# A graph step and a mixture of experts in one kernel: ScalarE's follow-up steps up to a slot later, x loads three slots sooner

## The chip, the cores and the metric

The kernel runs on one core of one Trainium2 chip. The metric is device time in microseconds (us) of one execution. TensorE (PE) multiplies matrices, with the weight loads shown as PEld; VectorE (DVE) does elementwise work, reductions and scans; ScalarE (ACT) does activations and copies; GpSimd (POOL) issues the indirect transfers; SyncE (SP) issues most of the plain ones. Each engine executes its own list of instructions strictly in the order in which the program emitted them, so an instruction that waits holds up everything behind it on that engine.

## The reference, cut to what matters

There are 6250 nodes with 256 features, and 100,000 edges with 96 features, sorted by target node. The first half adds a graph step to x, the second half a mixture of experts with two of sixteen experts per node.

```python
h1 = layernorm(x)
s   = segment_sum(edge, dst); m = segment_max(edge, dst); mean = s / max(count, 1)
h   = concat([h1, s, m, mean, u[0]])
x   = x + h1 + relu(h @ W1 + b1) @ W2 + b2
t   = layernorm(x)
val, idx = top_k(t @ gate_w + gate_b, 2);  w = softmax(val)
moe = sum_k w[k] * (relu(t @ w1[idx[k]] + b1[idx[k]]) @ w2[idx[k]] + b2[idx[k]])
out = x + layernorm(t + moe) * gamma + beta
```

With two choices the softmax needs one exponential of the difference of the two best logits (`dv`).

## The kernel before, in words

**Groups and slots.** The nodes are cut into 13 groups of four tiles of 125 nodes (the first group has two). One group's life is spread over slots; group g's multi-layer perceptron starts at slot B = 12 g. A list of tasks `(slot, function)` is sorted once, and that order is the order of emission for all engines. A slot is a place in this list, with a planned length of 4.6 us; it is no time on the chip.

**The edge stream.** Sums and maxima over the edges are no tasks but a generator (`steps`, `edge_stream`) that is drawn from between slots while the planned time allows (`credit`). It cuts the edges into seven regions and those into chunks. For each chunk SP loads edges (`raw`, three buffers, L176), VectorE forms running sums and maxima into `rw` (four operations of 125x768 per step, L316 to L320), and SP stores them to DRAM (`rows_d`, L329). After a region its last rows must be chained: `chain_runs` has three parts. `over_runs` (L385 to L396) chains the eight runs in a partition into the tile `ct`, of which there is one buffer; ScalarE copies the last run into it (L392). `to_features` transposes on TensorE (L404, L406), `over_partitions` scans on VectorE (L415 to L421), `to_partitions` transposes back (L430), `to_runs` adds the carry (L436, L438), and POOL stores `ct` as `carry_d` (L440). Functions given to `for_pe` are kept back until the next slot begins.

**One group around the change.** SP loads x (`take_x`, L680) at slot B-17. VectorE takes mean and variance (`stats_x`, L690, L691), ScalarE the root (`root_x`, L696), VectorE its inverse (`scale_x`, L702), ScalarE normalises (`norm_x`, L710). POOL gathers edge rows (`take_edges`, L730) and carries (`take_carry`, L737) for four tiles, VectorE joins them (`join_edges`, L743, L745), ScalarE scales them (L750, L617, L618), TensorE transposes (`turn`, L763) through a single bank `pT`, and ScalarE copies each out (`inT`, L764). `hidden` (L772, L789) is followed by ScalarE's relu (L794), `output` (L800) by VectorE's `residual` (L805 to L810). Then come the second root (`root_b`, ScalarE, L814), its inverse (`scale_b`, L820), the transposes `turn_b` (L830, copied out by ScalarE as `gT`, L831), `logits` (L838), `choose` on VectorE (L845 to L852) with the exponential on ScalarE at its end (L853), `rank`, `rank_2` (L873, L874), `place` (L882 to L895, which reads the exponential at L891), and `send` (POOL, L899), which scatters the rows to the experts' lists.

**Experts.** After the last group the rows are taken in blocks of 256: up to 14 blocks of one expert first, then 43 others (L1166 and L1190 are the two layers, L1172 and L1170 the relu, L1089 and L1091 the weighting).

**Queues.** SP's queue holds edge loads, stores of rows and x loads in the order of emission. POOL's queue holds the gathers of `blk_i` (L495, which need VectorE's L490 to L492), the sends, the stores of carries and the gathers of rows and carries.

The exponential and the square root belong to different function tables of ScalarE; the program holds a table load (`ACT_TABLE_LOAD`) wherever the table changes, 28 in all.

Of the kernel before, what the change touches and what calls it, by code (L numbers as in the profile page):

```python
# [13 lines left out]
AF = mybir.ActivationFunctionType  # L14
# [7 lines left out]
RR = 8  # L22
# [15 lines left out]
SLOTS = 12  # L38
# [7 lines left out]
def kernel(  # L46
# [18 lines left out]
    nc = tc.nc  # L65
    N, D = x.shape
    E, EF = edge.shape
# [23 lines left out]
    GRP = [(GS * (NG - 1 - g), GS * (NG - 1 - g) + (GS if g else N0)) for g in range(NG)]  # L91
# [126 lines left out]
    early = w1p.tile([P, 2 * WE * EF], F32, name="w1")  # L218
# [117 lines left out]
    def for_pe(fn):  # L336
        deferred.append((clock[0], fn))

    def tell_pe(now=False):

        while deferred and (now or deferred[0][0] < clock[0]):
            deferred.pop(0)[1]()
            told[0] = -1 if now else clock[0]

    def edge_stream():

        parts, of = [], 0

        def next_part():
            for cost in parts.pop(0)():  # L350
                yield cost
            stored[of] = not parts

        def ready():
            return not deferred and (clock[0] < 0 or told[0] < clock[0])

        for cost, whole, end in steps():
            yield cost
            if whole and parts and ready():
                yield from next_part()  # L360
            if end is not None:
                while parts:
                    tell_pe(True)
                    yield from next_part()
                parts, of = chain_runs(end), end
                yield from next_part()
                while parts and end == 0:
                    tell_pe(True)
                    yield from next_part()
        while parts:  # L370
            while not ready():
                yield None
            yield from next_part()
# [4 lines left out]
    def chain_runs(c):  # L378
        prev = prevs.pop(c)
        ct = chp.tile([P, RR, 2 * EF], F32, name="ct")  # L380
        kb, kp, kb2 = (chp.tile([P, RR], F32, name=nm) for nm in ("kbar", "kp", "kbar2"))

        def over_runs():

            nc.vector.tensor_scalar(kb, kall[:, c], 2.0, -1.0, op0=OP.mult, op1=OP.add)  # L385
            nc.vector.tensor_scalar(kb, kb, BIG, None, op0=OP.mult)
            nc.vector.tensor_tensor_scan(kp[:, ::-1], kall[:, c, ::-1], kall[:, c, ::-1], 1.0, op0=OP.mult, op1=OP.min)
            nc.vector.tensor_scalar(kb2, kp, 2.0, -1.0, op0=OP.mult, op1=OP.add)
            nc.vector.tensor_scalar(kb2, kb2, BIG, None, op0=OP.mult)
            run = tuple(a[:, RR - 1, :] for a in prev)  # L390
            for h in range(2):
                nc.scalar.copy(ct[:, RR - 1, h * EF:(h + 1) * EF], run[h])  # L392
            for r in reversed(range(RR - 1)):
                to = ct[:, r, 0:EF], ct[:, r, EF:]
                nc.vector.scalar_tensor_tensor(to[0], run[0], kall[:, c, r:r + 1], prev[0][:, r, :], op0=OP.mult, op1=OP.add)
                nc.vector.scalar_tensor_tensor(to[1], run[1], kb[:, r:r + 1], prev[1][:, r, :], op0=OP.min, op1=OP.max)  # L396
                run = to
                if r % 3 == 0:
                    yield 1.8
            for_pe(to_features)  # L400

        def to_features():
            over_runs.pk = pk = eps.tile([EF, 3, P], F32, name="ps")
            nc.tensor.transpose(pk[:, 0, :], kp[:, 0:1].to_broadcast([P, EF]), ident[:P, :P])  # L404
            for h in range(2):
                nc.tensor.transpose(pk[:, 1 + h, :], ct[:, 0, h * EF:(h + 1) * EF], ident[:P, :P])  # L406

        def over_partitions():
            pk = over_runs.pk
            st = chp.tile([EF, 2, P + 1], F32, name="st", bufs=2)  # L410
            for h in range(2):
                if chain[0] is None:
                    nc.vector.memset(st[:, h, P:], 0.0)
                else:
                    nc.vector.tensor_copy(st[:, h, P:], chain[0][:, h, 0:1])  # L415
            kk = chp.tile([EF, 2, P], F32, name="kk")
            nc.vector.tensor_copy(kk[:, 0, :], pk[:, 0, :])
            nc.vector.tensor_scalar(kk[:, 1, :], kk[:, 0, :], 2.0, -1.0, op0=OP.mult, op1=OP.add)
            nc.vector.tensor_scalar(kk[:, 1, :], kk[:, 1, :], BIG, None, op0=OP.mult)
            for h in range(2):  # L420
                nc.vector.tensor_tensor_scan(st[:, h, P - 1::-1], kk[:, h, ::-1], pk[:, 1 + h, ::-1], st[:, h, P:],  # L421
                                             op0=(OP.mult, OP.min)[h], op1=(OP.add, OP.max)[h])
            chain[0] = st
            yield 2.0
            for_pe(to_partitions)

        def to_partitions():
            over_runs.pc = pc = eps.tile([P, 2 * EF], F32, name="ps")
            for h in range(2):
                nc.tensor.transpose(pc[:, h * EF:(h + 1) * EF], chain[0][:, h, 1:], ident[:EF, :EF])  # L430

        def to_runs():
            tmp = chp.tile([P, RR, EF], F32, name="tmp")
            for h, k, o0, o1 in ((0, kp, OP.mult, OP.add), (1, kb2, OP.min, OP.max)):
                cs = ct[:, :, h * EF:(h + 1) * EF]
                nc.vector.tensor_tensor(tmp, over_runs.pc[:, None, h * EF:(h + 1) * EF].to_broadcast([P, RR, EF]),  # L436
                                        k[:, :, None].to_broadcast([P, RR, EF]), op=o0)
                nc.vector.tensor_tensor(cs, cs, tmp, op=o1)  # L438
                yield 1.9
            nc.gpsimd.dma_start(carry_d[EP * c:EP * (c + 1)].rearrange("(p r) f -> p r f", p=P), ct)  # L440

        return [over_runs, over_partitions, to_runs]


# [230 lines left out]
    G = [{} for _ in GRP]  # L675
# [165 lines left out]
    def choose(g):  # L841
        n = GRP[g][1] - GRP[g][0]
        lg = gtp.tile([P, GS, NE], F32, name="lg")
        G[g]["V8"], G[g]["I8"] = V8, I8 = gtp.tile([P, GS, 8], F32, name="V8"), gtp.tile([P, GS, 8], U32, name="I8")
        nc.vector.tensor_tensor(lg[:, :n], G[g]["pL"][:, :n * NE].rearrange("p (i e) -> p i e", e=NE),  # L845
                                G[g]["xt"][:, :n, D + 5:D + 6].to_broadcast([P, n, NE]), op=OP.mult)
        nc.vector.tensor_tensor(lg[:, :n], lg[:, :n], gbs[:, None, :].to_broadcast([P, n, NE]), op=OP.add)
        for i in range(n):
            nc.vector.max(V8[:, i, :], lg[:, i, :])
            nc.vector.max_index(I8[:, i, :], V8[:, i, :], lg[:, i, :])  # L850
        G[g]["dv"] = dv = gtp.tile([P, GS], F32, name="dv")
        nc.vector.tensor_sub(dv[:, :n], V8[:, :n, 1], V8[:, :n, 0])  # L852
        nc.scalar.activation(dv[:, :n], dv[:, :n], AF.Exp)  # L853

    def rank(g):
        a, z = GRP[g]
# [356 lines left out]
    def at_slot(T, fn, *a, cost=0.0):  # L1213
        tasks.append((T, len(tasks), fn, a, cost))

    stream = edge_stream()
    cuts = []

# [11 lines left out]
    for g, (a, z) in enumerate(GRP):  # L1230
        B, n = SLOTS * g, z - a
# [4 lines left out]
    for g, (a, z) in enumerate(GRP):  # L1236
        B, n = SLOTS * g, z - a
        if g:
            if g > 1:
                at_slot(max(0, B - 17), take_x, g)  # L1240
                after = 5 if g == GW else 0
                at_slot(B - 14 + after, stats_x, g, 0, cost=1.2)
                at_slot(B - 13 + after, stats_x, g, 1, cost=1.2)
# [4 lines left out]
            for i in range(n):  # L1248
                if g >= GW:
                    late = 3 if g == GW else 0  # L1250
# [19 lines left out]
        for i in range(n):  # L1270
            at_slot(B + HC + 1 + i, residual, g, i, cost=1.1)
        early = GS - n
        at_slot(B + SLOTS + 1 - early, root_b, g)
        at_slot(B + SLOTS + 2 - early, scale_b, g, cost=0.3)
        late = 0 if g >= NG - 2 else 1
        for k in range(DC):
            at_slot(B + SLOTS + 1 + k, turn_b, g, k)
        at_slot(B + SLOTS + 3 + late, logits, g)
        at_slot(B + SLOTS + 4 + late, choose, g, cost=2.4)
        at_slot(B + SLOTS + 5 + late, rank, g, cost=1.3)  # L1280
        at_slot(B + SLOTS + 6 + 2 * late, rank_2, g)
        at_slot(B + SLOTS + 7 + 2 * late, place, g, cost=1.5)
        for i in range(n):
# [20 lines left out]
    for b in range(GW, len(IB)):  # L1304
# [11 lines left out]
        early = 0 if b == GW else 2  # L1316
# [80 lines left out]
    with tc.If(bad_v != 0):  # L1397
# [7 lines left out]
        for lo in range(0, N, NC):  # L1405
# [18 lines left out]
            for n0 in range(0, min(NC, N - lo), P):  # L1424
                n = min(P, NC - n0, N - lo - n0)
# [14 lines left out]
    with tc.manual_schedule():  # L1440
# [56 lines left out]
        for slot, _, fn, args, cost in tasks:  # L1497
            while slot > T:
# [6 lines left out]
                g = min(T // SLOTS, NG - 1)  # L1505
# [61 lines left out]
```

## Time and profile before

| what | value |
|---|---|
| median of three runs | 1291.13 us (1291.03 to 1294.33) |
| the profiled execution, its own time | 1299.43 us |
| its span, first to last instruction | 1297.6 us |
| PE / DVE / ACT / POOL busy over the span | 1113.4 / 963.4 / 612.6 / 558.8 us |
| mean granted clock of TensorE | 0.955 |
| PE and DVE busy from 110 to 728 us, out of 618 | 538.9 and 547.1 us |
| PE and DVE busy from 728 to 806 us, out of 78 | 76.4 and 23.8 us |

The profiled execution took 8.3 us longer than the median of the other three. The span falls into the preparation (to about 110 us), the groups with the edge stream (to about 728 us), the last groups without it (to about 806 us) and the experts. In the tables a line such as `ACT dv L853 <- DVE dv L852: 75.2, 8, 16.2` says that ScalarE sat idle before line 853 until VectorE's line 852 had ended, 75.2 us in total, 8 times, at most 16.2 us. In the timeline, `[4.97 <-DMA ...]` is the idle time before an instruction and what ended it.

### The profile page before, as it was taken

The page shows a single profiled execution, that of the slowest core. Times are in us where ns is not written, and L with a number is a line of the kernel's source. Part 1 is how long each engine was busy: PE and PEld are TensorE (multiplying, and loading weights), DVE is VectorE, ACT ScalarE, POOL GpSimd, SP SyncE. Part 2 cuts the span into 40 slices and gives each one's busy share as a digit, 9 for nine tenths or more (in the row PEclk, how much of TensorE's full clock was granted, in tenths as well). Part 3 has the DMA queues.
Part 4 walks back from the last instruction along what each step waited for, and adds up shares of the span by engine and source line. Part 5 has one row for each costly group of instructions (what it writes and reads, how often), then busy time and mean ns, then how long its engine had stood idle before and what let it go on. Part 6 is the DMA issues. An engine that isn't in the chain of part 4 may idle for free.

```text
span 1297.6 us, 16883 instructions
## 1 busy us (share of the span) xinstructions
PE 1113.4 (86%) x4637; PEld 783.4 (60%) x4637; DVE 963.4 (74%) x2754; ACT 612.6 (47%) x1449; POOL 558.8 (43%) x721
## 2 busy tenths in 40 slices
PE   2484796998789989899989999998999998989992
PEld 1252363655455554646646566886888777778881
DVE  4569787988988979999989422444377777778885
ACT  3484253662437542343424422432466666656662
POOL 4121142663347645375263333030145554545664
PEclk9897898999889998999999999998999999999996
DMA  5948785797779998898997331231677777778972
GB/s 163 209 108 234 206 242 160 204 242 208 216 222 267 252 244 228 235 255 228 274 260 237 90 95 42 66 100 50 195 229 228 231 238 252 254 228 254 280 259 73
DMA packets 179475, 261.25 MB, mean 201 GB/s; under 512 B 35915, under 2 KB 145963, under 8 KB 173729
## 3 DMA queue, kind: packets, MB, share of 16 engines
q1 hardware_dynamic: 140241, 202.23, 54.4%
q0 software_dynamic: 39008, 57.35, 16.1%
q8 instruction: 40, 0.66, 0.2%
q14 instruction: 74, 0.61, 0.2%
q10 hardware_dynamic: 112, 0.41, 0.1%
HBM read 146.70 MB, written 122.01 MB: 207 GB/s over the span
## 4 chain that ended last, share of the span: by engine, by line
PE 35%; DVE 13%; ACT 3%; DMA 3%; issue 3%; POOL 1%; POOLq 0%; SPq 0%; ACTq 0%; DVEq 0%
PE acc L1190 14%; PE acc L1166 11%; PE acc L772 5%; PE acc L800 3%; DVE yb L1089 2%; ACT yb L1091 2%; DVE rw L320 1%; DVE rw L317 1%; DVE rw L319 1%; DVE rw L316 1%; DMA xt<-in_x_dram 1%; ACT hb L1172 1%; DMA cg<-carry_d,next_i 1%; DMA xg_d<-xt,pos_i 1%; POOL xg_d L899 1%
## 5 line engine op out<-in xcount | busy, mean ns | idle before, releaser
L772 PE MATMUL acc<-inT,w1x 128*128 128x500 f32 (+1 forms) x832 | 369.0, 592 | 8.9 <-DVE xt L805 8.9
L772 PEld LDWEIGHTS acc<-inT,w1x 128*128 128x128 f32 x832 | 159.0, 199 | 169.7 <-issue 151.9
L1166 PE MATMUL acc<-xT,wt 128*128 128x256 f32 x912 | 223.2, 388 | 29.3 <-ACT hb L1172 25.7
L899 POOL DMA_INDIRECT xg_d<-xt,pos_i x100 | 134.4, 1344 | 250.2 <-DVE xt L895 119.8
L1190 PE MATMUL acc<-wt,hb 128*128 128x256 f32 x912 | 207.1, 380 | 0.0
L1166 PEld LDWEIGHTS acc<-xT,wt 128*128 128x128 f32 x912 | 169.2, 191 | 62.3 <-ACT hb L1172 38.1
L1190 PEld LDWEIGHTS acc<-wt,hb 128*128 128x128 f32 x912 | 174.1, 191 | 23.9
L800 PE MATMUL acc<-w2s,hT 128*125 128x256 f32 x800 | 186.5, 388 | 0.0
L800 PEld LDWEIGHTS acc<-w2s,hT 128*125 128x125 f32 x800 | 150.5, 193 | 23.7 <-issue 1.9
L1102 POOL DMA_INDIRECT g<-y_d,from_i x86 | 91.8, 1067 | 120.8 <-DMA y_d<-yb 90.5
L1135 POOL DMA_INDIRECT out_dram<-g,to_i x86 | 89.1, 1036 | 102.7 <-ACT hb L1172 86.5
L1091 ACT ACTIVATE yb<-yb,w_b 128x256 f32<-128x256 f32 x114 | 51.7, 501 | 154.0 <-DVE yb L1089 147.8
L495 POOL DMA_INDIRECT gb<-in_dst_dram,blk_i x50 | 74.1, 1483 | 114.2 <-issue 59.4
L1172 ACT ACTIVATE hb<-acc,wt 128x256 f32<-128x256 f32 x200 | 87.7, 464 | 49.5 <-PE acc L1166 41.0
L1089 DVE TENSOR_TENSOR yb<-acc,xe 128x512 f32<-128x512 f32 x57 | 39.4, 691 | 88.3 <-PE acc L1190 57.4
L794 ACT ACTIVATE hT<-acc,c 128x500 f32<-128x500 f32 (+1 forms) x104 | 60.1, 660 | 71.4 <-PE acc L789 71.4
L319 DVE TENSOR_TENSOR rw<-rw,raw 125x768 f32<-125x768 f32 x88 | 83.8, 953 | 0.0
L320 DVE TENSOR_TENSOR rw<-rw,raw 125x768 f32<-125x768 f32 x88 | 83.7, 951 | 0.0
L316 DVE TENSOR_TENSOR rw<-rw,keep 125x768 f32<-125x768 f32 x81 | 76.8, 948 | 5.0 <-DMA rows_d<-rw 4.9
L317 DVE TENSOR_TENSOR rw<-rw,bar 125x768 f32<-125x768 f32 x81 | 77.0, 950 | 0.0
L730 POOL DMA_INDIRECT at<-rows_d,first_i x44 | 61.6, 1399 | 34.2 <-issue 21.5
L737 POOL DMA_INDIRECT cg<-carry_d,next_i x44 | 63.2, 1437 | 25.7 <-issue 11.3
(313 smaller groups left out, 1577.9 us busy)
## 6 DMA issues: line engine op xcount, KB each, us to landing
wt<-in_wpack_dram SPq DMA_DIRECT2D x44, 1026.0 KB
rows_d<-rw SPq DMA_DIRECT2D x46, 960.0 KB
rows_d<-rw SPq DMA_DIRECT2D x46, 540.0 KB
raw<-in_edge_dram SPq DMA_DIRECT2D x46, 480.0 KB
xb<-xg_d SPq DMA_DIRECT2D x57, 263.0 KB
y_d<-yb SPq DMA_DIRECT2D x57, 256.0 KB
raw<-in_edge_dram SPq DMA_DIRECT2D x46, 270.0 KB
xt<-in_x_dram SPq DMA_DIRECT2D x12, 500.0 KB
```

Source lines behind the costliest of these rows:

```text
L316: nc.vector.tensor_tensor(su, prev[0], keep[c][:, :, s + j, None].to_broadcast(bcast), op=OP.mult)
L317: nc.vector.tensor_tensor(mx, prev[1], bar[c][:, :, s + j, None].to_broadcast(bcast), op=OP.min)
L319: nc.vector.tensor_tensor(su, su, x_j, op=OP.add)
L320: nc.vector.tensor_tensor(mx, mx, x_j, op=OP.max)
L772: nc.tensor.matmul(G[g]["pH"][m % 4][:, :n * P], w1x[:, k, m * 128:(m + 1) * 128], inT[:, k, :n * P], start=(k == 0), stop=False)
L800: nc.tensor.matmul(pO, G[g]["hT"][m][:, i * P:(i + 1) * P], w2s[:, m, :], start=(m == 0), stop=(m == HC - 1))
L899: d = nc.gpsimd.indirect_dma_start(out=xg_d[:, :], out_offset=IndirectOffsetOnAxis(ap=G[g]["pos"][:, i, k:k + 1], axis=0), in_=G[g]["xt"][ ...
L1102: d = nc.gpsimd.indirect_dma_start(out=g[:, h, :].bitcast(I32), out_offset=None, in_=y_d[:, :], in_offset=IndirectOffsetOnAxis(ap=BL[b]["f ...
L1135: d = nc.gpsimd.indirect_dma_start(out=out[:, :], out_offset=IndirectOffsetOnAxis(ap=BL[b]["to"][:, h:h + 1], axis=0), in_=g[:, h, :], in_ ...
L1166: nc.tensor.matmul(pB[i][:, half, :], wt[:, k * FF + m * 128:k * FF + (m + 1) * 128], xT[:, k, :], start=(k == 0), stop=(k == DC - 1))
L1172: nc.scalar.activation(hb[:, m, :], pB[i][:, half, :], AF.Relu, bias=bias)
L1190: nc.tensor.matmul(pY[:, h, :], hb[:, m, h * 128:(h + 1) * 128], wt[:, W2O + m * D:W2O + (m + 1) * D], start=(m == order[0]), stop=(m == o ...
```

## The change

Four things move, and nothing is added or taken away on any engine.

- The exponential leaves `choose` and becomes a task of its own, `choose_2`, one slot later in most groups (after `rank`, and half a slot further).
- `root_b` and `scale_b` come one slot later.
- The copies of the last run into `ct` leave `over_runs` and stand at the head of `to_features`, which is emitted when the next slot begins. For the third region (index 2) the first part of the chain is no longer emitted at once, but at the next whole step of the stream.
- `take_x` is listed at slot B-20 instead of B-17.

```diff
                 parts, of = chain_runs(end), end
-                yield from next_part()
+                if end != 2:
+                    yield from next_part()
@@ over_runs
             run = tuple(a[:, RR - 1, :] for a in prev)
-            for h in range(2):
-                nc.scalar.copy(ct[:, RR - 1, h * EF:(h + 1) * EF], run[h])
@@
         def to_features():
+            for h in range(2):
+                nc.scalar.copy(ct[:, RR - 1, h * EF:(h + 1) * EF], prev[h][:, RR - 1, :])
@@ choose
-        nc.scalar.activation(dv[:, :n], dv[:, :n], AF.Exp)
+
+    def choose_2(g):
+        n = GRP[g][1] - GRP[g][0]
+        nc.scalar.activation(G[g]["dv"][:, :n], G[g]["dv"][:, :n], AF.Exp)
@@ the list of tasks
-                at_slot(max(0, B - 17), take_x, g)
+                at_slot(max(0, B - 20), take_x, g)
@@
-        at_slot(B + SLOTS + 1 - early, root_b, g)
-        at_slot(B + SLOTS + 2 - early, scale_b, g, cost=0.3)
+        at_slot(B + SLOTS + 2 - early, root_b, g)
+        at_slot(B + SLOTS + 3 - early, scale_b, g, cost=0.3)
@@
         at_slot(B + SLOTS + 5 + late, rank, g, cost=1.3)
+        at_slot(B + SLOTS + 5 + late + (0.5 if late else 0), choose_2, g)
```

## The prediction

> **What bounds the kernel now.** I read the stages first (busy time by stretch), then who waited for whom in the stretch that the change touches, then the timeline around each wait. The stages, with PE, PEld, DVE, ACT and POOL busy and the instruction counts in brackets:
>
> ```profile
> 110.00:728.00 618.00, 538.89 (x2031) 321.14 (x2030) 547.10 (x1451) 260.49 (x605) 294.47 (x281) 0.94 0.84 229
> 728.00:806.00 78.00, 76.38 (x309) 48.75 (x309) 23.76 (x107) 23.41 (x46) 28.03 (x40) 1.00 0.23 67
> ```
>
> From 728 us TensorE is full and nothing else matters. From 110 to 728 us TensorE and VectorE are both near nine tenths. The waits decide which leads. First VectorE's, then TensorE's and ScalarE's, all from 110 to 728 us:
>
> ```profile
> DVE at L743 <- DMA cg<-carry_d,next_i: 23.6, 14, 5.4
> DVE bsa L690 <- DMA xt<-in_x_dram: 9.7, 2, 5.0
> DVE ct L395 <- DMA carry_d<-ct: 7.7, 1, 7.7
> DVE rw L316 <- DMA rows_d<-rw: 4.9, 2, 4.3
> DVE tmp L436 <- PE ps L430: 1.5, 2, 0.9
> DVE kk L417 <- PE ps L406: 0.6, 2, 0.4
> ```
>
> ```profile
> PE pT L763 <- ACT inT L764: 22.1, 8, 7.7
> PE ps L406 <- DVE ct L395: 13.6, 3, 9.8
> ...
> PE acc L772 <- DVE xt L805: 8.9, 2, 4.7
> ```
>
> ```profile
> ACT dv L853 <- DVE dv L852: 75.2, 8, 16.2
> ACT xt L814 <- DVE mvb L810: 64.2, 10, 11.8
> ```
>
> ScalarE's long waits are what the change aims at, but idle ScalarE costs nothing by itself. TensorE does lose time to it (22.1 us). VectorE, however, waits for TensorE only 2.1 us (1.5 + 0.6) in 618 and never for ScalarE; all its other waits, 45.9 us, are for transfers. So VectorE leads this stage, and TensorE's gaps are mostly slack that it would spend waiting for VectorE a little later. I therefore price the change by VectorE's waits. Three lines of its timeline are touched:
>
> ```profile
> 221.41 0.32 DVE L395 SCALAR_TENSOR_TENSOR ct<-rw,kall 125x96 f32<-125x96 f32 x1 [7.74 <-DMA carry_d<-ct]
> ...
> 374.85 0.43 DVE L690 BATCH_NORM_STATS2 bsa<-xt 125x6 f32<-125x256 f32 x1 [4.97 <-DMA xt<-in_x_dram]
> ...
> 654.28 0.43 DVE L690 BATCH_NORM_STATS2 bsa<-xt 125x6 f32<-125x256 f32 x1 [4.73 <-DMA xt<-in_x_dram]
> ```
>
> **The change part by part.**
>
> *Third region's chain.* VectorE wants to write `ct` at 213.67 while the previous carry is still being stored. In the changed order the region's marks (L246 to L249, 224.63 to 225.39, 0.76 us), one step of the next region (L316 to L320, 225.39 to 228.89, 3.50 us) and the moved L820, L821 (0.25 us) stand ahead, so the wait falls from 7.74 by 4.5 to 3.2 us. What is late next is the join of the carries. POOL's gathers there start only when the same store has landed:
>
> ```profile
> 221.66 1.20 POOL L737 DMA_INDIRECT cg<-carry_d,next_i  x1 [7.97 <-DMA at<-rows_d,first_i]
> ...
> 229.48 1.20 POOL L737 DMA_INDIRECT cg<-carry_d,next_i  x1 [0.30 <-issue]
> ```
>
> Where VectorE waited for a gather, it came 6.7 us (285.81 to 292.54) to 11.0 us (463.72 to 474.74) after its issue. The fourth, issued at 229.48, can land at 236.2 at the earliest; its join was at 237.75. So 0 to 1.5 us remain of the 4.5; I take 0.8, the middle. TensorE's 9.79 us before 224.53 shrink too, under VectorE's pace.
>
> *x loads.* On SP's queue of the changed program nine of the ten x loads issued from 172.82 us on stand earlier by one pair of edge load and row store, the one at 360.39 by two; the one at 232.33 keeps its place. The load at 360.39 is then issued after the store that ended near 340.6, about 20 us sooner, and it landed 14.5 us after issue: the 4.97 us go. Late next is POOL: its gathers of `blk_i` at 376.78 had idled 3.76 us for VectorE, behind a send that ended at 372.94:
>
> ```profile
> 372.94 0.09 POOL L904 MEMSET gap<- 1x1 f32 x1
> 376.78 1.69 POOL L495 DMA_INDIRECT gb<-in_dst_dram,blk_i  x1 [3.76 <-DVE blk_i L492]
> ```
>
> From there POOL runs without a gap to the last gather (issued at 410.54), whose join VectorE waits for at 417.95. POOL can move up by 3.5 us at most (376.78 to about 373.25), so the join's wait grows by 1.5. I take 3.5; ends 0 and 5.0. The load at 638.98 moves ahead of the edge load at 631.28, 7.7 us sooner. It took 15.3 us; it would land near 646.6, and VectorE wants it at 649.55. All 4.73 us go, with 3 us to spare; ends 0 and 4.7. Is TensorE able to follow? It idled 4.18 us before 657.55 (waiting for that same VectorE) and 1.54 us at 688.29 (the exponential); 5.7 us against 4.7, so yes. The edge load pushed behind x loses x's issue time, 1.5 to 2.2 us on SP; it is consumed two chunks later, and VectorE shows no wait for `raw` anywhere, so 0. The cover is those two chunks, some 20 us; gone, it would cost the same 2 us per load.
>
> *Exponential.* 13 of 0.2 us and 13 table loads of 1.28 us move behind `keep_x` and two copies, and stand just before the relu L794. Of TensorE's gaps, 7.66 (351.31), 0.79, 4.02 (469.30), 4.17 (531.64) and 1.54 us came from copies queued behind it, 18.2 us. They go, and VectorE sets the pace again: 0 on the path; ends 0 and a gain of 2.1 us, VectorE's whole wait for TensorE. A new wait is added for the relu: in the group at 466 us VectorE's `dv` ended at 466.09 and TensorE's L789 at 465.27, so the relu would start near 466.3, still sooner than its 469.65; the other groups look alike. `place` reads the exponential (L891) about 20 us later. In the last group it moves one block later, to about 835.5; L891 is at 844.10.
>
> *Second root.* The square-root table load now stands before L696 instead of L814, after the first `gT` copy. L696 ends some 2 us later, and L702, which needs it, came 3.2 us or more later than that would be (203.06 against 199.9; 614.61 against 609.8). L820 moves down VectorE's list with it; in the last two groups it waits inside idle time (14.58 us before 774.05, 2.54 before 820.48). 0.
>
> *ct copies.* 14 of 0.27 us; TensorE's 2.60 us at 425.68 and 1.16 at 284.76 go, under VectorE's pace. 0; ends 0 and 1.
>
> Two pages bear on this. The Trainium skill, "ScalarE: Activation LUTs", section on what ACT_TABLE_LOAD costs, gives 1283 ns for the load, which the trace has, and a drain of some 1380 ns besides; here L814 started 1.30 us after its load did (808.55, 809.85), so no drain follows it. With the drain L702's margin would be 1.8 us instead of 3.2, and the sum the same. The skill's "DMA: Bandwidth & Descriptors", section "Issuing engines are not separate DMA queues", says that transfers of SP and GpSimd interleave on the same engines, which speaks against moving x loads into the gathers' time; no row separates the two, and with an estimated 2.1 us per load (500 KB at 240 GB/s) at five joins the sum would lose its 9.0 us.
>
> Sum: 0.8 + 3.5 + 4.7 = 9.0 us. Against the profiled execution that is 1299.4 to 1290.4; it took 8.3 us more than the median, so against the median, 1291.1 - 9.0 = 1282.1 us.
>
> **The rivals.**
> - *All of the waits go.* POOL and the gathers keep up, and 7.74 + 4.97 + 4.73 + 2.1 = 19.5 us are gained: 1271.6. For it: VectorE lacks other reasons to wait. Against it: the joins hang on POOL, as shown.
> - *The joins take it all.* Each microsecond gained comes back at L743, or only the last x load counts partly: a gain of 0 to 3.9 us, 1287 to 1291. For it: 14 waits for gathers already. Against it: most are anchored in VectorE's own work (carry store at 451.73, index at 514) and move along.
> - *Slower: x loads delay the gathers.* Place: the joins at 175.5, 288 to 296, 412 to 418, 475 to 479 and 536, the five groups where VectorE waits now. A gather took 6.7 to 11.0 us; if an earlier x load puts each last one at the slow end, that is up to 4.3 us x 5 = 21.5, and 1291.1 - 9.0 + 21.5 = 1303.6. Above 1.8 us per join (9.0 / 5) it decides. For it: the load at 292.76 moves to about 283, among the gathers issued at 279.77 to 287.32. Against it: x loads at 172.82, 292.76, 410.37, 468.88 and 535.12 fall into such times already, and leave them sooner.
> - *Not as it says*: only the load at 232.33 keeps its place, and nobody waits for it.
>
> **How the numbers follow.** Three runs before lie within 3.3 us, so under 0.3%, 3.9 us, is no change. Forecast (a gain of 4 to 14 us) 0.58; more than that 0.17; the joins take it all 0.13; slower 0.12. Likeliest case by itself: 1277 to 1287. The range for 8 in 10 reaches to 1272, the full gain, and to 1294, which takes 12 of the 21.5 us of contention. Faster 0.75, same 0.13, slower 0.12.
>
> **What would show it.** After: no VectorE wait for `xt`; the one at L395 near 3 us; TensorE's wait for L764 under 6 us; VectorE's for gathers 24 to 28 us, the stage's end near 797 instead of 806, and the experts unchanged. The prediction is wrong if VectorE's waits for gathers or `raw` grow by more than 9 us, or if TensorE turns out to wait at the relu.

## The result and the profile after

The changed kernel takes 1293.85 us (median of 20 runs, 1286.62 to 1299.51), the kernel before 1289.56 us (median of 20, 1285.34 to 1294.42). The ratio is 1.0029, with a 95% interval of 1.0015 to 1.0043: 0.29% slower, at the edge of what I had called no change, where 9.0 us or 0.7% faster was forecast. The time lies just inside the range's upper end of 1294; that is luck, for the range reached there for contention at the gathers, and the loss arose in other places too.

The profiled execution after took 1290.32 us (span 1288.5), less than that of before (1299.43). This is no gain: the first matmul of the experts (L1170) starts at 809.79 us, where it was 805.08, so the groups' stage is 4.7 us longer and the experts happened to take 478.7 us instead of 492.5. I therefore compare the two traces up to the experts only.

VectorE's waits from 110 to 728 us after the change (engine, line and tile, who was waited for: us in total, times, longest):

```profile
DVE at L744 <- DMA cg<-carry_d,next_i: 33.8, 14, 5.3
DVE rw L316 <- DMA rows_d<-rw: 11.8, 5, 4.9
DVE ct L394 <- DMA carry_d<-ct: 4.1, 1, 4.1
DVE tmp L437 <- PE ps L431: 1.5, 2, 0.9
DVE kk L418 <- PE ps L407: 1.2, 2, 0.7
DVE rw L316 <- DVE rw L320: 0.3, 1, 0.3
```

The waits that the change aims at did go: none is left for `xt` (9.7 before), and the one for the carry's store fell from 7.7 to 4.1 us. Together 13.3 us. In their place the gathers' waits grew by 10.2 us (23.6 to 33.8) and those for stored rows by 6.9 (4.9 to 11.8). The sum of all waits is 52.7 us; it was 48.2.

TensorE's waits in the same stretch:

```profile
PE pT L764 <- ACT at L751: 14.4, 15, 2.4
PE acc L801 <- ACT hT L795: 12.0, 5, 5.0
...
PE pT L764 <- ACT inT L765: 4.5, 5, 2.3
```

The wait for the copies of transposes fell from 22.1 to 4.5 us, as forecast. But 12.0 us of it came back at the relu (L795), and the scaling of the edge rows (L751) now holds TensorE for 14.4 us. The stages of the changed kernel (PE, PEld, DVE, ACT, POOL busy, clock, share of the DMA engines, GB/s):

```profile
110.00:728.00 618.00, 538.05 (x2011) 317.99 (x2011) 547.64 (x1452) 257.87 (x596) 292.19 (x278) 0.95 0.84 228
728.00:806.00 78.00, 78.00 (x315) 49.03 (x312) 21.81 (x101) 27.99 (x55) 30.93 (x43) 1.00 0.27 73
```

Nothing in the first row moved by more than 3.2 us. The column that I had printed before and not used is the last but one: the DMA engines are busy for 84% of the stretch.

**Where the time comes and goes.** In VectorE's timeline of the changed kernel, these are the places that decide:

```profile
178.61 0.32 DVE L744 SCALAR_TENSOR_TENSOR at<-cg,cross,at 125x96 f32<-125x96 f32 x1 [5.10 <-DMA cg<-carry_d,next_i]
...
224.82 0.32 DVE L394 SCALAR_TENSOR_TENSOR ct<-rw,kall 125x96 f32<-125x96 f32 x1 [4.08 <-DMA carry_d<-ct]
...
241.83 0.32 DVE L744 SCALAR_TENSOR_TENSOR at<-cg,cross,at 125x96 f32<-125x96 f32 x1 [5.26 <-DMA cg<-carry_d,next_i]
...
404.25 0.96 DVE L316 TENSOR_TENSOR rw<-rw,keep 125x768 f32<-125x768 f32 x1 [1.00 <-DMA rows_d<-rw]
...
681.24 0.96 DVE L316 TENSOR_TENSOR rw<-rw,keep 125x768 f32<-125x768 f32 x1 [4.94 <-DMA rows_d<-rw]
```

One profile is one execution, so I take the same instructions in all the profiles of the kernel before (four) and of the changed one (three) that the experiments below gave as well. The time of each is counted from the first step of the edge stream (110.79 us before, 111.22 after), and the table shows by how much it differs from the mean of the four profiles of before:

| VectorE's instruction, its time in the profile of before | four of before | three of after | mean after |
|---|---|---|---|
| first join, 175.51 | +0.1, +1.1, -1.0, -0.1 | +2.7, +2.4, +4.3 | +3.1 |
| step behind the first join, 176.44 | -1.0, +0.8, +0.4, -0.2 | +2.9, +3.1, +5.1 | +3.7 |
| step behind the third region's chain, 230.91 | -1.0, +0.8, +0.4, -0.3 | -2.3, -2.0, -0.2 | -1.5 |
| third join of the next group, 237.29 | -1.0, +0.8, +0.4, -0.2 | +3.1, +2.8, +5.4 | +3.8 |
| step before the first late x load, 358.05 | -1.2, -0.2, +0.2, +1.2 | +4.6, +2.6, +4.7 | +4.0 |
| statistics of that x, 374.85 | -0.9, -0.1, -0.3, +1.3 | -0.1, -2.1, -0.1 | -0.8 |
| step behind the next four joins, 420.15 | -1.3, +1.4, -0.8, +0.7 | +1.3, +0.6, +2.1 | +1.3 |
| step before the second late x load, 637.70 | -3.5, +2.2, +0.8, +0.5 | 0.0, +1.4, +4.6 | +2.0 |
| statistics of that x, 654.28 | -1.9, +1.6, +1.6, -1.2 | -3.3, -1.8, +1.4 | -1.2 |
| step whose buffer waits for its store, 676.52 | -2.9, +1.9, +1.0, +0.1 | +1.4, +1.3, +5.8 | +2.8 |
| TensorE's last output of the groups, 803.03 | -3.1, +1.7, +0.9, +0.5 | +1.2, +1.1, +5.7 | +2.7 |

Each gain is in the table, and each is followed by a loss. 3.1 us are lost at the first join (3.7 by the step behind it). The third region's chain gains 5.2 (3.7 to -1.5) and loses 5.3 six us later at the third join. The first x load gains 4.8 and gives 2.1 back. The second gains 3.2 and gives 4.0 back. The last rows by themselves overlap between the kernels (the stage's end differs by 2.7 us, at a spread of 5), but the differences from row to row do not: from 654.28 to 676.52 us the three profiles of after lose 3.0 to 4.7 us, and the four of before between -1.0 and +1.3.

### The profile page after: what moved, and what is told of

It is laid out like the page before. It is cut to its first block, busy times and chain, and to the rows that moved or that the text cites. A ratio compares the mean times of both kernels' runs of the same rounds, so it can differ in the third digit from the quotient of the medians.

```text
span 1288.5 us, 16892 instructions
## 1 busy us (share of the span) xinstructions
PE 1119.7 (87%) x4637; PEld 784.8 (61%) x4637; DVE 964.0 (75%) x2754; ACT 613.8 (48%) x1449; POOL 559.7 (43%) x721
## 4 chain that ended last, share of the span: by engine, by line
PE 32%; DVE 14%; DMA 4%; ACT 4%; issue 3%; POOL 1%; SPq 1%; POOLq 0%; DVEq 0%; ACTq 0%
PE acc L1194 14%; PE acc L1170 10%; PE acc L773 4%; DVE yb L1093 2%; PE acc L801 2%; DMA rows_d<-rw 2%; ACT yb L1095 2%; DVE rw L320 2%; DVE rw L319 2%; DVE rw L317 1%; DVE rw L316 1%; ACT hb L1176 1%; DMA cg<-carry_d,next_i 1%; DMA xg_d<-xt,pos_i 1%; ACT rsc L1124 1%
## 5 line engine op out<-in xcount | busy, mean ns | idle before, releaser
L773 PE MATMUL acc<-inT,w1x 128*128 128x500 f32 (+1 forms) x832 | 361.2, 581 | 5.2 <-DVE xt L806 5.2
L773 PEld LDWEIGHTS acc<-inT,w1x 128*128 128x128 f32 x832 | 156.3, 196 | 163.1 <-issue 145.0
L1170 PE MATMUL acc<-xT,wt 128*128 128x256 f32 x912 | 224.6, 390 | 13.4 <-ACT hb L1176 7.7
L801 PE MATMUL acc<-w2s,hT 128*125 128x256 f32 x800 | 196.4, 401 | 12.0 <-ACT hT L795 12.0
L1170 PEld LDWEIGHTS acc<-xT,wt 128*128 128x128 f32 x912 | 170.3, 192 | 46.4 <-ACT hb L1176 23.8
L1194 PEld LDWEIGHTS acc<-wt,hb 128*128 128x128 f32 x912 | 174.6, 191 | 23.9
L801 PEld LDWEIGHTS acc<-w2s,hT 128*125 128x125 f32 x800 | 154.2, 199 | 41.4 <-ACT hT L795 17.1
L795 ACT ACTIVATE hT<-acc,c 128x500 f32<-128x500 f32 (+1 forms) x104 | 60.1, 660 | 77.2 <-PE acc L790 77.2
L765 ACT COPY inT<-pT 128x500 f32<-128x500 f32 (+1 forms) x65 | 36.2, 557 | 113.4 <-PE pT L764 113.4
L316 DVE TENSOR_TENSOR rw<-rw,keep 125x768 f32<-125x768 f32 x81 | 77.0, 951 | 12.1 <-DMA rows_d<-rw 11.8
L731 POOL DMA_INDIRECT at<-rows_d,first_i x44 | 64.4, 1463 | 35.5 <-issue 22.8
```

What stands on the lines that cost most here:

```text
L316: nc.vector.tensor_tensor(su, prev[0], keep[c][:, :, s + j, None].to_broadcast(bcast), op=OP.mult)
L773: nc.tensor.matmul(G[g]["pH"][m % 4][:, :n * P], w1x[:, k, m * 128:(m + 1) * 128], inT[:, k, :n * P], start=(k == 0), stop=False)
L801: nc.tensor.matmul(pO, G[g]["hT"][m][:, i * P:(i + 1) * P], w2s[:, m, :], start=(m == 0), stop=(m == HC - 1))
L1170: nc.tensor.matmul(pB[i][:, half, :], wt[:, k * FF + m * 128:k * FF + (m + 1) * 128], xT[:, k, :], start=(k == 0), stop=(k == DC - 1))
L1194: nc.tensor.matmul(pY[:, h, :], hb[:, m, h * 128:(h + 1) * 128], wt[:, W2O + m * D:W2O + (m + 1) * D], start=(m == order[0]), stop=(m == o ...
```

## The experiments

**One part at a time, whole kernel.** The theories at this point: (1) earlier x loads push edge loads and row stores on SP's queue into the gathers' time; (2) the loss comes from ScalarE's steps and the third region's chain, which move VectorE against GpSimd. Four kernels: the kernel before with the x loads alone; the changed one without them; the latter with the third region's chain begun as before; the kernel before with only the two loads that were waited for.

```
e1_x_only    -  at_slot(max(0, B - 17), take_x, g)
(of before)  +  at_slot(max(0, B - 20), take_x, g)
e2_no_x      -  at_slot(max(0, B - 20), take_x, g)
(of after)   +  at_slot(max(0, B - 17), take_x, g)
e3_act_only  as e2_no_x, and
             -  if end != 2:
             -      yield from next_part()
             +  yield from next_part()
e4_x_two     -  at_slot(max(0, B - 17), take_x, g)
(of before)  +  at_slot(max(0, B - (20 if g in (6, 11) else 17)), take_x, g)
```

> Kernel before, with the x loads at slot B-20 and nothing else. Theory 1 (the earlier x loads push edge loads and row stores on SP's queue into the gathers' time): VectorE's 9.7 us of waits for xt go, its waits for gathers and stored rows grow by 12 us or more, and the time is 2 to 7 us longer (ratio 1.0015 to 1.0055). Theory 2 (the loss comes from ScalarE's steps and the third region's chain, which move the joins against POOL; the x loads gain what was forecast): gathers' waits stay at 23 to 26 us, time 4 to 9 us shorter (0.993 to 0.997).

> Changed kernel with the x loads back at slot B-17; ScalarE's moves and the third region's chain remain. Theory 1: the waits for xt are back at about 9.7 us, gathers' waits at about 24 us; time within 2 us of the kernel before or up to 3.7 us shorter (0.997 to 1.0015). Theory 2: gathers' waits stay near 34 us and the time is 8 to 14 us longer than before (1.006 to 1.011), since what the x loads gain is missing as well.

> Changed kernel with the x loads back at slot B-17 and the third region's chain begun at once as before: only the exponential, the second root and the two copies into ct are moved. Theory 1: TensorE's waits for the copies of transposes fall from 22 to about 5 us and VectorE does not move, so the time is the same (0.9985 to 1.0015). Theory 2: TensorE's new waits at the relu and at the scaling of the edge rows (12 and 9 us more) reach VectorE; 4 to 10 us longer (1.003 to 1.008).

> Kernel before, with only the two x loads moved that VectorE waits for (groups 6 and 11, issued at 360.39 and 638.98), both two or one pair of edge load and row store earlier. Theory 1: the waits for xt go as in the changed kernel; nothing else shifts before 340 us, so most of the gain stays: 3 to 6 us shorter (0.9953 to 0.9977) unless the second one is eaten again by the wait for stored rows at 681 us (then 2 to 4 us, 0.997 to 0.9985). Theory 2: both are kept, 7 to 9 us shorter (0.993 to 0.9945).

Measured against the kernel before on the same chip (median 1297.10 us, 1285.35 to 1306.46): x loads alone 1.0014 [0.9983, 1.0045], without them 1.0015 [0.9985, 1.0046], ScalarE's steps alone 1.0014 [0.9977, 1.0051], the two loads 0.9992 [0.9958, 1.0026]. The intervals are as wide as the effect, so that no part's cost can be read from these times. But theory 2's values for the x loads alone (0.993 to 0.997), for the kernel without them (1.006 to 1.011) and for the two loads (0.993 to 0.9945) all lie outside: the earlier x loads do not bring the forecast gain even by themselves. The waits that had been expected came only in part. With the x loads alone, the waits for gathers and stored rows together grew by 11.3 us (39.8 against 28.5), near the 12 of theory 1; without them, the wait for `xt` came back as 2.9 us and not 9.7, and the waits for gathers were 31.2 us, between theory 1 (24) and theory 2 (34).

**The groups' stage alone.** Since the experts vary by more than the change, both kernels were cut behind the groups. The blocks of the experts, their tables and the final stage are left out:

```
+  left_out = (norm_block, turn_block, run_block, count_all, table_rest, table_rest_2, open_final)
+  tasks[:] = [t for t in tasks if t[2] not in left_out]
   tasks.sort(key=lambda t: t[:2])
...
-  for b in range(NA, NS):
-      run_block(b, NS)
-  run_rest(NS)
+  last = xall[:, (NG - 1) % XB]
+  nc.sync.dma_start(out[0:P * GS].rearrange("(i p) d -> p i d", p=P), last[:, :, 0:D])
```

> Kernel before, cut behind the groups: the experts' blocks, their tables and the final stage are left out, and one group's rows are written as output, so that the groups' stage is timed without the experts, whose share differed from run to run by more than the change (492.5 and 478.7 us in the profiles of before and after). Both theories: about 820 to 860 us, and single times within 3 us of each other, against 20 us in the whole kernel; this is the base for the other cut kernels.

> Changed kernel, cut in the same way (experts left out). Both theories: 3 to 6 us longer than the cut kernel before, as the first expert matmul came 4.7 us later in the whole kernel.

> Kernel before with the x loads at slot B-20, cut in the same way (experts left out). Theory 1 (x loads contend): 4 to 7 us longer than the cut kernel before. Theory 2 (ScalarE's steps and the third region's chain cost): 4 to 9 us shorter.

> Changed kernel with the x loads back at slot B-17, cut in the same way (experts left out). Theory 1: within 1.5 us of the cut kernel before. Theory 2: 6 us longer or more. If both parts cost and don't add up (each moves the joins against the stores of rows, and the later wait swallows the earlier one): 2 to 4 us longer, with the x loads alone at 4 to 7 us as well.

The cut kernels before and after were run again later, unchanged, as bases for what follows:

> The cut kernel before once more, unchanged (experts left out), as the base on the same chip and to pool with the first: 834 to 843 us by all theories.

> The cut kernel before (experts left out), unchanged, as the base on the same chip: 836 to 843 us by all theories.

> The cut changed kernel (experts left out), unchanged, again: 3 to 6 us longer than the cut kernel before, if the difference of the whole kernels arises before the experts; within 1.5 us of it if not.

The three sets of before have medians of 839.43, 841.75 and 839.90 us (16 runs, 834.46 to 843.51, mean 839.9); the two of after 842.36 and 844.37 (12 runs, 838.69 to 851.06, mean 844.7). The difference of the means is 4.7 us, with a 95% interval of about 1.5 to 8.0 from the spread of the runs. It agrees with the 4.3 us of the whole kernels: the loss arises before the experts. The single times spread by 9 us, not 3 as I had expected, so the stage itself varies.

The x loads alone have a mean of 842.2 us (5 runs, median 842.87), the changed kernel without them 841.6 (6 runs, median 841.87). Each is some 2 us above the base, with 95% intervals of -1.9 to 6.4 and -3.0 to 6.4 us. That excludes the gain of 4 to 9 us that theory 2 wanted for the x loads alone; theory 1 (4 to 7 and within 1.5) and the third reading, that both parts cost, can't be told apart by these times. The waits show the exchange more plainly than the times. First the cut kernel before, from 110 to 728 us:

```profile
DVE at L743 <- DMA cg<-carry_d,next_i: 28.7, 15, 3.7
DVE ct L395 <- DMA carry_d<-ct: 8.6, 1, 8.6
DVE bsa L690 <- DMA xt<-in_x_dram: 7.4, 2, 4.8
DVE rw L316 <- DMA rows_d<-rw: 6.5, 3, 4.2
```

Then the x loads alone:

```profile
DVE at L743 <- DMA cg<-carry_d,next_i: 30.7, 16, 5.2
DVE rw L316 <- DMA rows_d<-rw: 13.0, 5, 4.5
DVE ct L395 <- DMA carry_d<-ct: 8.0, 1, 8.0
```

And the changed kernel without them:

```profile
DVE at L744 <- DMA cg<-carry_d,next_i: 31.2, 15, 4.7
DVE bsa L691 <- DMA xt<-in_x_dram: 9.4, 2, 6.5
DVE rw L316 <- DMA rows_d<-rw: 7.2, 5, 4.5
DVE ct L394 <- DMA carry_d<-ct: 5.0, 2, 3.4
```

The waits for stored rows follow the x loads (6.5 and 7.2 without, 13.0 with), the wait for `ct` follows the third region's move (8.6 and 8.0 without, 5.0 with), and the sum stays: 53.3, 54.5 and 55.1 us with the small waits counted, and 52.6 in the cut kernel after. What is taken from one wait comes back in another. Two cautions: the profiled executions themselves took 842.15, 843.38, 844.78 and 838.69 us, so the sums go with the execution that was profiled and not with the medians; and over all profiles the stored rows' waits are 4.9 to 9.0 us with the x loads where they were and 7.9 to 14.2 with all or two of them earlier, so that the two ranges touch (7.9 is the whole kernel with the x loads alone).

**Is it the place on SP's queue, or the transfers themselves?** Theory 3 says that the DMA engines are short, so that what is moved earlier delays something else whatever queue it is on. Three kernels: 5 MB more that nobody waits for; the early x loads from ScalarE's queue; the early x loads with less data.

```
c_extra (of c_before)    +  if g > 2:
                         +      nc.scalar.dma_start(out[a * P:z * P], x[a * P:z * P])
c_x_act (of c_x_only)    -  nc.sync.dma_start(xt[:, :z - a, 0:D], ...)
                         +  queue = nc.scalar if g > 2 else nc.sync
                         +  queue.dma_start(xt[:, :z - a, 0:D], ...)
c_x_small (of c_x_only)  +  m = 1 if g > XB else z - a
                         -  nc.sync.dma_start(xt[:, :z - a, 0:D], x[a * P:z * P]...)
                         +  nc.sync.dma_start(xt[:, :m, 0:D], x[a * P:(a + m) * P]...)
```

> Cut kernel before (experts left out), and ScalarE's queue issues beside each of the ten x loads from group 3 on a copy of the same 500 KB from x to the output, which nobody reads or waits for; no engine's work changes. Theory 1 (it is the place on SP's queue that costs): within 2 us of the cut kernel before. Theory 3 (the DMA engines themselves are short from 150 to 690 us, and a removed wait comes back as another one): 5 MB at the 229 GB/s of this stage are 22 us of transfers, of which gaps take some, so 8 to 22 us longer, with VectorE's waits for gathers and stored rows that much larger.

> Cut kernel with the x loads at slot B-20 (experts left out), issued from ScalarE's queue instead of SP's, so that no edge load or row store stands behind them. Theory 1: VectorE's wait for stored rows falls from 13 to about 6.5 us, none for xt, and the time is 4 to 9 us shorter than with the loads on SP's queue (834 to 838 against 842.9). Theory 3: same bytes at the same time, so the waits for gathers and stored rows stay near 44 us together and the time at 840 to 845 us.

> Cut kernel with the x loads at slot B-20 on SP's queue (experts left out); from group 6 on only one of the four tiles is loaded (the other three keep old data, so what is computed from them is not the reference's), 2.6 MB less in seven loads. Theory 1: each load still stands ahead of edge load and row store but holds the queue for less; 0 to 4 us shorter than with whole loads (839 to 843). Theory 3: 2.6 MB at 229 GB/s are 11 us of transfers less; 4 to 11 us shorter (832 to 839), and the waits at 404 and 681 us for stored rows under 1 us.

Medians beside 841.75 us of the cut kernel before on the same chip (6 runs each): 846.55 with 5 MB more, 846.46 from ScalarE's queue, 837.67 with less data. By the means, and with 95% intervals, that is 5.1 us longer (0.9 to 9.4), 4.6 longer (0.7 to 8.5) and 4.2 shorter (-0.3 to 8.7). So 5 MB unread cost about 4.8 us, which speaks against theory 1 (it allowed 2) without excluding it. The wait that grew is not one of those that theory 3 had named; it is the one for x, beside whose loads the copies are issued. First the base, then with 5 MB more:

```profile
DVE bsa L690 <- DMA xt<-in_x_dram: 8.1, 2, 4.2
...
DVE bsa L692 <- DMA xt<-in_x_dram: 13.3, 3, 8.3
```

The waits for gathers and stored rows are 31 and 32 us there. From ScalarE's queue the loads are no cheaper; theory 1 wanted 834 to 838. The waits of that kernel, in an execution of 839.76 us, its fastest of six:

```profile
DVE rw L316 <- DMA rows_d<-rw: 23.9, 9, 6.2
DVE at L744 <- DMA cg<-carry_d,next_i: 14.7, 10, 2.8
```

There is no edge load behind the x load on its queue now, and still VectorE waits for the stores of rows, for 23.9 us instead of 13.0; the gathers are waited for less. It is not quite "the same time", as the expectation had it: ScalarE comes to these instructions sooner, and the loads start 2 to 25 us before those on SP's queue (149.9 against 170.1 us for the first, 614.8 against 639.4 for the one before the store at 681 us). The wait at that store is down to 0.3 us, and another of 6.2 us stands at 627.8, behind the load at 614.8, where SP needs 6.13 us to issue a store, although no x load stands on its queue:

```profile
621.21 6.13 SPq L329 DMA_DIRECT2D rows_d<-rw  x2
```

With the other queue the loss changes its place. This is what the Trainium skill says under "DMA: Bandwidth & Descriptors", in the section "Issuing engines are not separate DMA queues": queues of different engines share the same transfer engines. The prediction had weighed it and set it aside; here the runs agree with it.

Theory 3 has the right sign in all three, though with less data the interval still holds 0, and it is wrong in size. It wanted 8 to 22 us for the 5 MB (22 us of transfers at 229 GB/s) and got 4.8: most of the extra traffic costs nothing. With 2.6 MB less, the wait at 680 us was to vanish, but it is there with a quarter of the bytes:

```profile
680.57 0.96 DVE L316 TENSOR_TENSOR rw<-rw,keep 125x768 f32<-125x768 f32 x1 [3.41 <-DMA rows_d<-rw]
```

So most of the x load's own bytes are not needed for this wait. SP's timeline shows the side of the store that frees the buffer. Before:

```profile
165.92 3.59 SPq L176 DMA_DIRECT2D raw<-in_edge_dram  x2
...
661.02 2.23 SPq L176 DMA_DIRECT2D raw<-in_edge_dram  x2
663.29 2.34 SPq L329 DMA_DIRECT2D rows_d<-rw  x2
```

After:

```profile
165.61 1.72 SPq L681 DMA_DIRECT2D xt<-in_x_dram  x1
...
167.43 10.85 SPq L176 DMA_DIRECT2D raw<-in_edge_dram  x2
...
660.09 6.15 SPq L176 DMA_DIRECT2D raw<-in_edge_dram  x2
666.28 4.17 SPq L329 DMA_DIRECT2D rows_d<-rw  x2
```

The edge load is issued 0.9 us sooner than before and takes 6.15 us to issue instead of 2.23, so the store behind it starts 3.0 us later, although VectorE had its rows ready sooner. With three buffers it is, by count, the store that the step at 681.24 waits for. From the start of that edge load VectorE needs about 15.5 us to the step (15.5 in the four profiles of before, 15.5 to 16.8 where x is earlier), so it does not come sooner by this clock; the store comes later. Edge load and store together take SP 4.6 to 8.7 us to issue in the four profiles of before and 7.6 to 11.0 in the eight with the full x load earlier, and where VectorE waits, the step starts 9.1 to 12.2 us after the store's issue has ended. The ranges overlap, and two profiles of before wait here as well (2.2 us, after 5.11 us for the edge load, and 1.2 us): the wait was near already. The share of the DMA engines is 1.01 from 670 to 690 us (1.02 before). At the first join the effect is clear: the edge load behind the early x load needs 10.85 us to issue (3.59 before, where it stood ahead), and 9.9 to 10.9 in all six profiles with this order and whole edge loads, against 2.5 to 4.8 in the twelve with the other. The join there waits 5.10 us instead of 3.11. The early loads may not be all of that loss: behind this join, VectorE is 2.5 and 3.4 us late with the x loads alone, but 2.6 and 0.0 with ScalarE's steps and the third region's chain alone.

**Room on the DMA engines.** If the transfers are the limit, the change must pay with fewer of them. From the tenth chunk on, the light kernels issue only the smaller half of each edge load. The work of the computing engines is unchanged; SP issues 40 transfers fewer, and the three `raw` buffers are declared as one tile cut in three.

```
-  raw = EP_["raw"].tile([P, RR, JS, EF], F32, name="raw")
+  raw = EP_["raw"][:, i % JB]
...
-  for o, i_ in halves(raw[:, :, :n], src[:, :, s:s + n]):
+  for o, i_ in halves(raw[:, :, :n], src[:, :, s:s + n])[1 if i > 8 else 0:]:
```

> Cut kernel before (experts left out) with light edge loads: from the tenth chunk on only the 45-partition half of each edge load is issued, the other 80 partitions keep old edges (so sums and maxima are not the reference's); some 40 loads of 240 to 480 KB, about 18 MB, are missing, and all engines' work stays. Theory 3 (DMA engines short): 18 MB are 80 us of transfers at 229 GB/s; VectorE's waits fall from 51 us to under 25 and the time by 15 to 40 us. Theory 4 (something else paces the stage): under 10 us shorter.

> Changed kernel, cut and with light edge loads in the same way (experts left out, 80 of 125 partitions keep old edges). Theory 3: with room on the DMA engines the change does what was forecast, 3 to 9 us shorter than the light kernel before. Theory 4: 2 to 5 us longer than it, as in the pair with whole loads.

Measured: 835.44 us for the light kernel before (833.73 to 840.16), 830.89 for the light changed one (829.97 to 832.96; 5 runs each, no overlap). The change is 4.6 us faster there, and 4.5 us slower with whole loads on the same chip (844.37 against 839.90); by the means 5.3 faster (95% interval 2.0 to 8.7) and 5.6 slower (0.9 to 10.3). Its sign depends on the edge loads, which theory 4 does not allow. Whether it is their bytes or SP's time to issue them that matters, this pair can't say, since both are less. And theory 3 is only half right: 32 GB/s less in this stretch (197 instead of 229) made the kernel before 4.5 us shorter (by the means 2.9, -0.4 to 6.2) and not 15 to 40, and the waits did not fall under 25 us; on this theory 4 (under 10) was right. The light kernel before:

```profile
DVE at L743 <- DMA cg<-carry_d,next_i: 34.6, 13, 7.8
DVE ct L395 <- DMA carry_d<-ct: 7.2, 2, 7.0
DVE rw L316 <- DMA rows_d<-rw: 6.1, 2, 4.2
DVE bsa L690 <- DMA xt<-in_x_dram: 1.5, 1, 1.5
```

The light changed one:

```profile
DVE at L744 <- DMA cg<-carry_d,next_i: 23.9, 13, 4.0
DVE at L744 <- DMA at<-rows_d,first_i: 9.7, 2, 6.6
DVE rw L316 <- DMA rows_d<-rw: 6.4, 3, 4.3
...
DVE ct L394 <- DMA carry_d<-ct: 2.0, 1, 2.0
```

The wait for `xt` is nearly gone in the light kernel before already (1.5 us), and its place is taken by longer waits for gathers (34.6). So the gain is not the forecast one at its forecast places. The carry's store is waited for less (7.2 to 2.0), but at VectorE's instructions (one profile each, of 840.16 and 832.28 us) that gain of 4.3 us is lost again at the third join (4.2), as with whole loads. There the changed kernel is still 1.2 us behind; it is 2.5 us ahead at the statistics of the first late x, 7.1 ahead at 637.70 us, and no more at 676.52. So most of its lead arises at the joins between 237 and 638 us, and why they come sooner was not followed. The wait at 681 us, however, is absent from both light kernels, and waits for stored rows no longer grow with the change (6.1 and 6.4): that loss does need the edge loads.

**The two useful loads alone.**

> Cut kernel before (experts left out) with only the x loads of groups 6 and 11 at slot B-20. If the loss of the changed kernel comes from what is moved before the first join and in the third region, and the load of group 6 keeps its gain: 2 to 5 us shorter than the cut kernel before (835 to 838 against 840.0). If every removed wait comes back: 839 to 842.

> The whole kernel before with only the x loads of groups 6 and 11 at slot B-20, once more. If the gain of group 6 is kept: 2 to 5 us shorter (ratio 0.996 to 0.9985); if not, 0.999 to 1.001.

The cut kernel took 835.43 us (5 runs, 834.76 to 841.75), 4.0 to 6.3 us under the three bases, which ran on other chips (by the means 3.3 us, -0.3 to 7.0). Its waits:

```profile
DVE at L743 <- DMA cg<-carry_d,next_i: 23.4, 14, 3.5
DVE rw L316 <- DMA rows_d<-rw: 12.3, 4, 4.2
DVE ct L395 <- DMA carry_d<-ct: 8.4, 1, 8.4
```

The gathers' waits stay at the level of before, and those for stored rows grow as in the changed kernel. In its three profiles (both whole ones and the cut one) the statistics of the first x come 4.1 to 6.1 us sooner than the mean of before, and those of the second 5.9 to 9.2; at 676.52 us, behind the wait for the store (4.1 to 5.8 us), 1.2 to 6.0 are left. Nothing else is moved here, so this shows the exchange most plainly: the first load gains 4.8 us in each profile and gives 1.0 to 1.8 back by 420 us; the second gains 3.2 in each and gives 3.1 to 4.8 back at the store, that is, all of it. As a whole kernel it had 0.9987 [0.9963, 1.0012] the second time, after 0.9992. If it is faster than the kernel before, by what the first load keeps, these runs cannot show it; I know no version that is shown to beat both.

## Why the prediction was wrong

By its own steps, with the mean of the three profiles after against the four of before:

| step | forecast, us gained | measured |
|---|---|---|
| x loads beside the gathers, first join | 0 (rival: up to 4.3) | -3.1 (-3.7 by the step behind it) |
| third region's chain | 0.8 (0 to 1.5) | -0.1 (5.2 gained, 5.3 lost at the third join) |
| x load at 360.39 | 3.5 (0 to 5.0) | 2.7 (4.8, less 2.1 at stores and joins) |
| x load at 638.98 | 4.7 (0 to 4.7) | -0.8 (3.2, less 4.0 at the store) |
| exponential, root, `ct` copies | 0 | not resolved (1.0014 [0.9977, 1.0051]) |
| sum to the end of the groups | 9.0 | -2.7 in the profiles, -4.3 in the medians |

The stretches between the steps (0.2 us lost from 237 to 358 us, 0.7 from 420 to 638) make up the rest of the sum; they lie within the spread of the profiles.

*The step that failed most* is the second x load: "All 4.73 us go, with 3 us to spare". They went, but what is late next was looked for at TensorE alone, and was the store of rows: 3.2 us gained, 4.0 lost. The forecast had the queue in view ("The edge load pushed behind x loses x's issue time ... VectorE shows no wait for `raw` anywhere, so 0") and asked only whether the edge load would be late for its consumer, not what stands behind it on SP: the store, whose landing frees the buffer for L316. That wait was among the lines shown of before (4.9 us, twice).

*The second* is the term for contention, taken as 0. The rival "x loads delay the gathers" had the right sign and named the right first place, and its limit of 1.8 us per join was passed at 175.5 us (3.1). At the other four places its price did not show: in the profile after, the waits at 288 to 301 us are 8.6 us (7.4 before), at 412 to 421 us 5.8 (5.0), at 475 to 482 us 6.6 (6.7), at 536 to 539 us 0.9 (0.7). The forecast set the term to 0 because x loads fell among the gathers already; at the first join VectorE comes late where one goes out earlier. It is not the whole cause either; of the 13.3 us that went, the waits for stored rows took 6.9, the first join 2.0, and the third region's join 5.3, a little more than all of it.

*Third region.* The wait at the carry's store fell to 4.1 (forecast 3.2), and the join was rightly named as late next. But its room was counted from the fourth gather's issue at 229.48 at best; GpSimd issued the third and fourth at 231.13 and 233.25, because the carry's store before them was itself issued 2.8 us late, and the third gather took 10.7 us:

```profile
212.43 0.60 POOL L441 DMA_DIRECT2D carry_d<-ct  x1 [21.25 <-ACT hT L795]
...
231.13 1.82 POOL L738 DMA_INDIRECT cg<-carry_d,next_i  x1 [0.30 <-issue]
233.25 1.20 POOL L738 DMA_INDIRECT cg<-carry_d,next_i  x1 [0.30 <-issue]
```

So the chain's gain was lost in full, at the lower end of what was forecast (0 to 1.5). It does not take the early x loads: without them the chain gains 5.4 and 4.7 us and loses 5.7 and 4.3.

*Right* were the first x load (2.7 of 3.5 us kept), the vanished waits for `xt`, TensorE's wait at L764 (4.5, under 6), and that experts don't enter. *Wrong as a sign to look for*: the relu. It was to start sooner, and TensorE waited 12.0 us for it; VectorE's waits for TensorE rose only from 2.1 to 2.7 us, so this stayed off the path. Both signs that the prediction had named for being wrong thus appeared: TensorE waits at the relu, and the gathers' waits grew by 10.2 us, more than 9.

The root of it is the reading "VectorE leads". Its waits were all for transfers, and in its stretch the DMA engines were busy for 84%, 0.88 to 1.06 around the five joins where it waited. Removing a wait of such an engine brings it sooner to the next transfer. That the transfers come late because the DMA engines are full is not shown, though: after the change their share is 0.74 in the last 2.6 us before the first join and 0.69 from 236 to 242 us, while VectorE waits for the third. What sets the sum of VectorE's waits near 50 us is open: it was 47 to 57 us in all the cut kernels, also in the light kernel before with 32 GB/s less, so bytes alone don't set it; the chain of store, gather and join on GpSimd's queue is the other candidate, and was not tried by itself.

## What to carry to other kernels

When the leading engine waits only for transfers, a removed wait is worth what its next transfer lets through: walk on along that engine's list to the next wait for a DMA of any kind, stores that free buffers included, before a microsecond is counted. Read the DMA share of the stretch beside the busy engines; at 0.84 in the mean and about 1.0 around the waits, one earlier load here was paid for in full by a later store, one in part, and issuing them from another queue did not help. And where one stage varies by more than the effect, cut it out and time the rest: here the cut pair and the same instructions over several profiles showed what twelve runs of the whole kernel could not.

## What I had not expected of the hardware

- The time that SP needs to issue the same transfers varies threefold: two edge loads of 480 and 270 KB took 2.23 us to issue at 661 us before and 6.15 at 660 after; two of 240 and 135 KB took 3.59 us at 166 us before and 10.85 right behind an x load of 500 KB. What stands behind them on the queue is issued later by that difference.
- 5 MB of additional traffic cost 4.8 us (0.9 to 9.4), about a fifth of the 22 us that they need at the stage's 229 GB/s, and 19 MB less gained 4.5 us or less: at a mean share of 0.84, the price of a byte depends on where it falls.
- The same loads from ScalarE's queue, issued 2 to 25 us sooner, moved the waits from gathers to stores (30.7 and 13.0 us to 14.7 and 23.9) and left the time no better.
